# One hand-made instruction order across three stages, earlier page reads and split rotary angles in a two-layer block

## The chip, the core and the metric

The kernel runs on one core of one Trainium2 chip. The metric is the device time of one execution in microseconds (us). Everything is float32. PE is TensorE (matmul), DVE is VectorE, ACT is ScalarE, POOL is GpSimd, SP is SyncE; in this kernel SP does nothing but read a few indices and issue DMAs.

## The reference

There are eight sequences (B = 8) of 128 rows and 512 features. Layer 0 multiplies each sequence by one of eight adapter matrices and adds a small mixture of experts; layer 1 is an attention over a paged cache, followed by a gated bottleneck network. Cut to what matters here:

```python
# layer 0, per sequence b
c   = x[b] @ W0[adapter_id[b]].T
g   = c @ gate_w.T                       # 8 experts, the best 2, softmax
x1  = x[b] + c @ base_w.T + base_b + 2.0 * experts(c, g)

# layer 1, per sequence b
q, k, v = x1 @ Wq.T, x1 @ Wk.T, x1 @ Wv.T        # 32 query heads, 8 key heads, D = 128
pos     = cache_seqlens[b] + arange(128)
q, k    = rope(rmsnorm(q), pos), rope(rmsnorm(k), pos)   # cos/sin of pos * inv_freq
keys    = concat(k_cache[block_table[b]], k)     # 16 pages of 32 rows, then the new 128 rows
vals    = concat(v_cache[block_table[b]], v)
o       = softmax(q @ keys.T / sqrt(D), masked where cache row >= cache_seqlens[b]) @ vals
y       = o @ Wo.T
out     = x1 + gated_bottleneck(y)               # 64 gates, the best 16
```

## The kernel before

The program has three stages, each written in a `with` block of its own.

**Layer 0 (`l0`)** loops over the sequences, t = 0 to 7. In a pass PE multiplies by the adapter matrix (`l0_adapter`, L373, in two halves), DVE copies the result to `cT` (L382), PE multiplies `cT` by the gate and low-rank matrix `glw` (L390) and by `bww` (L395), DVE works out the gates (L401 to L419), and one pass later PE adds the experts (`l0_experts`, L437), DVE writes `x1` (L439), SP writes it to memory (`x1d`, L440) and PE transposes it (`l0_turn`, L447) into `x1T`. SP's queue loads, ahead of their pass, the adapter matrix `wt` (L284, three passes ahead), the transposed input `xT` and the input `xb`. In passes 2 to 7 SP also reads the cache pages of attention step 0 (`gather`, L151 for `kt` and L156 for `vt`), three pages a pass; a page is two DMAs of 64 KB. POOL's queue loads the projection weights (`load_q`, L129) and output weights (`load_o`, L134). After pass 1, `l0_angles` makes the rotary angles of all sequences on DVE (L345 to L361, ten instructions), and after pass 2 ACT makes `sin` and `cos` of them (L476, L477).

**Layer 1 (`l1`)** has 16 steps (a sequence and one half of the key heads) of four units each, 64 units. A unit is one key head with its four query heads. For a unit u: `project_q` (L195), `project_kv` (L208), `norms` (ACT's squares L224, POOL's `rs` L230), `rotate` (DVE, L242 to L255, into `ca`), a transposition (the first three units on PE, `transpose_qk` L634 with ACT's copy to `qkT` L638; the later ones through DVE and memory), `scores` (L660, L663), `mask_exp` (DVE L673, ACT L684), `normalize` (POOL L690), `blocks` (DVE L695), a transposition of the probabilities through memory (`exchange_out` L707 writes `px`, `exchange_in` L720 reads `pT`), `values` (L739) and `output` (L760). `make_mask` (DVE, L626) makes the mask of a step. Units 0 and 1 are projected and rotated at the end of `l0`; the first lines of `l1` are `transpose_qk(0)`, `project_q(2)`, `make_mask(0)`, `transpose_qk(1)`, `project_kv(2)`.

**The end (`l2`)** finishes the bottleneck network of the last sequences.

**What sets the order.** For SP's instructions one hand-made order holds for the whole program. For PE, DVE, ACT and POOL each of the first two stages has a hand-made order of its own (`l2` has one for PE, DVE and ACT), and where two stages meet a planner places the instructions. In the built program DVE's list at the seam of `l0` and `l1` reads: `mask` of step 0 (L626), then `rotate(0)`, then `rotate(1)`. An engine takes its list in order.

**Memory.** The tiles of `l1` (among them `mask` and `qkT`) take the place of the tiles of `l0`. So in the program's list of waits, `mask` of step 0 and `qkT` of unit 0 both wait for the last reader of that place, which is the DMA that writes `x1` of sequence 7 to memory (L440). `ca`, `rs`, `vn` and the tables lie elsewhere and have no such wait. SP's DMAs share eight semaphores in turn, so that an issue waits until the DMA eight before it has landed.

Of the kernel before, what the change touches and what calls it, by code (L numbers as in the profile page):

```python
# [9 lines left out]
F32 = mybir.dt.float32  # L10
I32 = mybir.dt.int32
AF = mybir.ActivationFunctionType
ALU = mybir.AluOpType
# [3 lines left out]
P = 128  # L17
B = 8
# [5 lines left out]
D = 128  # L24
HKV, REP = 8, 4
NH = REP + 1
PAGES, PSIZE, NPP = 64, 32, 16
# [16 lines left out]
PI_LOW = 3.1415925  # L44
INV_2PI = 0.15915494309189535
ROUND = 12582912.0

C1 = 6.28125
C2 = 0.0019340515136718750
C3 = 2.0 * PI - C1 - C2  # L50
# [3 lines left out]
def adaln_ffn_kernel(  # L54
# [23 lines left out]
):  # L78
    nc = tc.nc

    ctx.enter_context(tc.manual_schedule(engines={mybir.EngineType.SP}))
    const = ctx.enter_context(tc.tile_pool(name="const", bufs=1))
    keep = ctx.enter_context(tc.tile_pool(name="keep", bufs=1))
    wp = ctx.enter_context(tc.tile_pool(name="wp", bufs=GH))
# [9 lines left out]
    half_pi = const.tile([P, 1], F32, name="half_pi")  # L94
# [32 lines left out]
    def load_q(g, eng):  # L127
        t = wp.tile([P, NC, (REP + 2) * D], F32, tag="wqkv", name=f"wqkv_{g}")
        eng.dma_start(out=t, in_=wqkv[g].rearrange("(c p) n -> p c n", p=P))  # L129
        wq_t[g] = t  # L130
# [126 lines left out]


    with ExitStack() as l0:
        l0.enter_context(  # L260
            tc.manual_schedule(
                engines={
                    mybir.EngineType.PE,
                    mybir.EngineType.DVE,
                    mybir.EngineType.Activation,
                    mybir.EngineType.Pool,
                }
            )
        )
        w0p = l0.enter_context(tc.tile_pool(name="w0p", bufs=1))  # L270
        p2 = l0.enter_context(tc.tile_pool(name="l0_2", bufs=2))
        sm = l0.enter_context(tc.tile_pool(name="l0_s", bufs=2))
# [67 lines left out]
        fr = w0p.tile([P, D // 2], F32, name="fr")  # L340
        nc.gpsimd.dma_start(out=fr, in_=inv_freq.to_broadcast([P, D // 2]))

        def l0_angles():

            nc.vector.tensor_copy(lenf, leni)  # L345
            pos = w0p.tile([P, B], F32, name="pos")
            nc.vector.tensor_scalar(pos, lenf, pf, None, ALU.add)
            ang = yp.tile([P, B, D // 2], F32, tag="ya", name="ang")
            kk = yp.tile([P, B, D // 2], F32, tag="ya", name="kk")
            nc.vector.tensor_tensor(  # L350
                ang,
                pos.unsqueeze(2).to_broadcast([P, B, D // 2]),
                fr.unsqueeze(1).to_broadcast([P, B, D // 2]),
                ALU.mult,
            )
            nc.vector.tensor_scalar(kk, ang, INV_2PI, ROUND, ALU.mult, ALU.add)
            nc.vector.tensor_scalar(kk, kk, ROUND, None, ALU.subtract)
            for part in (C1, C2, C3):
                nc.vector.scalar_tensor_tensor(ang, kk, -part, ang, ALU.mult, ALU.add)
            nc.vector.tensor_scalar(ang, ang, PI_LOW, -PI_LOW, ALU.min, ALU.max)  # L360
            nc.vector.scalar_tensor_tensor(kk, ang, -1.0, ang, ALU.mult, ALU.max)  # L361
            return ang, kk

        state, cp_t, cT_t, lowT_t = {}, {}, {}, {}

# [88 lines left out]
        for t in range(B):  # L454
            l0_adapter(t, True)
            if t >= 1:
                l0_turn_low(t - 1)
            l0_adapter(t, False)
            if t + 3 < B:
                if t + 3 in (5, 6):  # L460
                    l0_home(t + 3)
                l0_load(t + 3)
            if t + 2 < B:
                l0_load_x(t + 2)
            if t >= 1:
                l0_experts(t - 1)
                if t in (3, 5, 7):
                    load_q((t - 3) // 2, nc.gpsimd)
            if t >= 2:
                gather(0, (t - 2) * 3, min((t - 1) * 3, NPP))  # L470
                l0_turn(t - 2)
            l0_base(t)
            if t == 1:
                angles = l0_angles()
            if t == 2:
                nc.scalar.activation(sin, angles[0], AF.Sin)  # L476
                nc.scalar.activation(cos, angles[1], AF.Sin, bias=half_pi, scale=-1.0)  # L477

        load_q(3, nc.gpsimd)
        for g in range(GH):  # L480
# [11 lines left out]
        project_kv(1)  # L492
        norms(1)
        rotate(1)
        gather(1, 0, 11)


    fw_t, zg_t = {}, {}
# [99 lines left out]


    with ExitStack() as l1:  # L600
        l1.enter_context(
            tc.manual_schedule(
                engines={
                    mybir.EngineType.PE,
                    mybir.EngineType.DVE,
                    mybir.EngineType.Activation,
                    mybir.EngineType.Pool,
                }
            )
        )  # L610
        wk1 = l1.enter_context(tc.tile_pool(name="l1_1", bufs=1))
        wk2 = l1.enter_context(tc.tile_pool(name="l1_2", bufs=2))
        pp = l1.enter_context(tc.tile_pool(name="l1_p", bufs=3))
# [203 lines left out]
        def iteration(u):  # L817

            on = lambda v: 0 <= v < NU
            fb = LAST.get(u)  # L820
            if on(u):
                st, k = units[u][0], units[u][1] % GH
                first, end = (0, 0, 6, 11)[k], (0, 6, 11, NPP)[k]
                if k > 0 and 1 < st + 1 < 2 * B:
                    gather(st + 1, first, first + 2)
            if on(u - 1):
                exchange_in(u - 1)
            if on(u) and k > 0 and 1 < st + 1 < 2 * B:
                gather(st + 1, first + 2, end)
            if u == 1:  # L830
                gather(1, 11)
            if on(u + 3) and units[u + 3][1] % GH == 0:
                make_tables(units[u + 3][0])
            if on(u - 1) and units[u - 1][1] == GH:
                load_y(units[u - 1][0])
            if on(u - 2):
                evict_o(u - 2)
            if u == NU:
                yT_t[fb] = f_turn(fb, *rooms[fb])
                z_turn(ORDER[0], bank("kv", "ztp_0"), rooms[ORDER[0]][0])  # L840
            if u == NU + 1:
                z_turn(ORDER[1], bank("q", "ztp_1"), rooms[ORDER[1]][0])
            for h in range(REP):
                if on(u):
                    scores(u, h)
                    mask_exp(u, h)
                    if h > 0:
                        normalize(u, h - 1)
                    if u == 1 and h == 1:

                        project_q(4)
                        transpose_qk(2)
                        project_kv(4)
                        rotate(3)
                        norms(4)
                    if h == 2:
                        new_pb(u)
                        if u + 2 in range(3, NU):
                            blocks_qk(u + 2, u)
                    if h > 1:  # L860
                        blocks(u, h - 2)
                    if h == 1 and u == NU - 3:
                        f_fold(rooms[fb][1])
                    if h == 2 and fb is not None:
                        yT_t[fb] = f_turn(fb, *rooms[fb])
                if on(u - 2):
                    output(u - 2, h)
            if on(u - 2):
                add_output(u - 2)
            if on(u + 1) and units[u + 1][1] % GH == 0:  # L870
                make_mask(units[u + 1][0])
            if on(u):
                normalize(u, REP - 1)
                blocks(u, REP - 2)
                blocks(u, REP - 1)
                exchange_out(u)
            if u == 0:
                project(3)
                rotate(2)
            elif u == 1:  # L880
                rotate(4)
            elif on(u + 3):
                project(u + 3)
                rotate(u + 3)
                if units[u + 3][0] == B - 1:
                    load_q(units[u + 3][1] + GH, nc.gpsimd)
            if u + 1 in range(3, NU):
                heads_qk(u + 1)
            if u == NU - 5:
                f_weights()  # L890
            if fb is not None:
                f_gate(fb, *f_project(fb, yT_t.pop(fb), *rooms[fb]), *rooms[fb])
            if on(u - 1):
                values(u - 1)
            if on(u - 2) and units[u - 2][0] == B - 1:
                load_o(units[u - 2][1] + GH, nc.gpsimd)
            if u in (NU - 3, NU - 2):
                load_y(B + u - (NU - 3))
            if NU - 4 <= u < NU:
                room(LAST[u + 1])  # L900
# [4 lines left out]
        transpose_qk(1)  # L905
        project_kv(2)
        norms(2)
        for u in range(NU + 2):
            iteration(u)


    with ExitStack() as l2:
        l2.enter_context(
            tc.manual_schedule(
                engines={
                    mybir.EngineType.PE,
                    mybir.EngineType.DVE,
                    mybir.EngineType.Activation,
                }
            )  # L920
        )
        p2 = l2.enter_context(tc.tile_pool(name="f_2", bufs=2))
        sm = l2.enter_context(tc.tile_pool(name="f_s", bufs=3))

# [152 lines left out]
```

## Time and profile before

| | |
|---|---|
| runs shown (3) | 1284.98 us median, 1283.83 to 1287.56 |
| profiled execution, its own time | 1285.63 us |
| its span, first to last instruction | 1283.9 us |
| PE busy | 1260.9 us (98%) |
| DVE busy | 783.3 us (61%) |
| ACT busy | 465.8 us (36%) |
| POOL busy | 342.0 us (27%) |
| mean granted TensorE clock | 0.997 |
| DMA | 293.15 MB, mean 228 GB/s |

The profile is one execution, 1.7 us of which lie around its span; it is 0.65 us above the median of the runs. A row of a timeline gives the start, the duration, the engine and line, the tiles (output <- inputs), how many instructions are merged, and in brackets the idle time of the engine before it and what ended that. "PEclk" is the TensorE clock that was granted, as a share of full speed. Matmuls are pipelined and their ends are modelled, so neighbouring rows overlap a little.

### The profile page before, as it was taken

Reading aid. Unit: us, or ns where it says so; the run is one execution under the profiler, and the core shown is the slowest. Engines: PE = TensorE matmul, PEld = TensorE weight load, DVE = VectorE, ACT = ScalarE, POOL = GpSimd, SP = SyncE. Lnnn points to the kernel's source line nnn. Section 1 sums busy time; section 2 is a strip of 40 time slices with the busy share of each in tenths; the row PEclk is TensorE's granted clock in tenths of the full one; section 3 lists DMA queues with packets and bytes.
Section 4 is the critical chain, followed back from the end, with each engine's and each line's share of the span. In section 5 each row is a group of like instructions: output and inputs, shape, how many; then the busy total and the mean of one; then the engine's idle time right before and its main releaser. Section 6 shows DMA issues by size and latency. Waiting matters only on the chain.

```text
span 1283.9 us, 15242 instructions
## 1 busy us (share of the span) xinstructions
PE 1260.9 (98%) x3949; PEld 670.4 (52%) x3949; DVE 783.3 (61%) x1794; ACT 465.8 (36%) x1397; POOL 342.0 (27%) x462
## 2 busy tenths in 40 slices
PE   8998999999999999999999999999999999999998
PEld 6665455555555555544555455555555555555545
DVE  3425666666666666656666566666666666665524
ACT  0214344334433443433343433433444444343211
POOL 2132232232323222323323222323232322221100
PEclk9999999999999999999999999999999999999999
DMA  8974667676767766699889776767767686786531
GB/s 307 305 269 123 215 208 240 198 248 226 221 217 239 228 219 223 228 284 294 277 267 291 231 232 226 236 226 224 246 215 233 207 260 204 234 276 214 187 107 49
DMA packets 176555, 293.15 MB, mean 228 GB/s; under 512 B 15971, under 2 KB 85924, under 8 KB 176468
## 3 DMA queue, kind: packets, MB, share of 16 engines
q1 hardware_dynamic: 153044, 218.83, 53.9%
q10 hardware_dynamic: 18960, 52.21, 11.7%
q0 software_dynamic: 4464, 21.14, 4.8%
q8 instruction: 31, 0.51, 0.2%
q14 instruction: 56, 0.46, 0.1%
HBM read 180.64 MB, written 111.48 MB: 228 GB/s over the span
## 4 chain that ended last, share of the span: by engine, by line
PE 88%; DMA 8%; DVE 2%; issue 1%; SPq 1%; POOL 0%; ACT 0%; ACTq 0%; DVEq 0%
PE o L739 21%; PE y L760 16%; PE s L660 15%; PE q L195 14%; PE kv L208 7%; DMA pT<-px 5%; PE s L663 4%; PE op L972 2%; PE bp L395 2%; PE cp L373 2%; DMA px<-pb 1%; PE fz L547 1%; PE fp L547 1%; DMA bww<-in_base_w 1%; PE cp L390 1%
## 5 line engine op out<-in xcount | busy, mean ns | idle before, releaser
L690 POOL TENSOR_SCALAR p<-p,den 128x640 f32<-128x640 f32 x256 | 204.3, 798 | 525.6 <-DVE den L689 525.6
L684 ACT ACTIVATE p<-p,low 128x640 f32<-128x640 f32 x256 | 212.1, 829 | 326.4 <-DVE den L689 231.4
L673 DVE CUSTOM_DVE_ANT_0 p<-s,mask,rs 128x640 f32<-128x640 f32 x256 | 226.2, 884 | 165.9 <-PE s L663 155.0
L760 PE MATMUL y<-wo,oT 128*128 128x512 f32 x512 | 261.4, 594 | 0.3 <-ACT oT L750 0.3
L660 PE MATMUL s<-kt,qkT 128*128 128x512 f32 x512 | 261.6, 592 | 0.0
L739 PE MATMUL o<-pT,vt 128*128 128x512 f32 x512 | 232.7, 597 | 7.7 <-DMA pT<-px 7.7
L195 PE MATMUL q<-wqkv,x1T 128*128 128x512 f32 x512 | 231.9, 596 | 0.0
L695 DVE STREAM_TRANSPOSE pb<-p 128x640 f32<-128x640 f32 x256 | 211.0, 824 | 11.7 <-POOL p L690 11.7
L663 PEld LDWEIGHTS s<-qkT 128*128 128x128 f32 x512 | 97.3, 190 | 122.5 <-issue 122.5
L195 PEld LDWEIGHTS q<-wqkv,x1T 128*128 128x128 f32 x512 | 97.6, 191 | 121.6 <-issue 121.6
L660 PEld LDWEIGHTS s<-kt,qkT 128*128 128x128 f32 x512 | 96.9, 190 | 118.8 <-issue 103.3
L739 PEld LDWEIGHTS o<-pT,vt 128*128 128x128 f32 x512 | 97.2, 191 | 108.3 <-issue 94.9
L224 ACT ACTIVATE sq<-q 128x128 f32<-128x128 f32 x256 | 71.0, 277 | 214.1 <-DVE pb L695 115.0
L242 DVE TENSOR_TENSOR ca<-q,tab 128x512 f32<-128x512 f32 x64 | 44.2, 690 | 165.0 <-ACT sq L224 162.0
L208 PE MATMUL kv<-wqkv,x1T 128*128 128x256 f32 x512 | 121.0, 379 | 0.0
L208 PEld LDWEIGHTS kv<-wqkv,x1T 128*128 128x128 f32 x512 | 97.0, 190 | 38.9 <-issue 29.0
L663 PE MATMUL s<-qkT 128*128 128x128 f32 x512 | 98.3, 274 | 0.0
L228 POOL TENSOR_SCALAR ss<-ss 128x5 f32<-128x5 f32 x64 | 12.6, 197 | 270.5 <-ACT sq L224 270.5
L750 ACT COPY oT<-o 128x512 f32<-128x512 f32 x64 | 37.4, 585 | 120.5 <-PE o L739 120.5
L760 PEld LDWEIGHTS y<-wo,oT 128*128 128x128 f32 x512 | 78.2, 192 | 3.6 <-issue 2.9
L230 POOL TENSOR_TENSOR rs<-ss,mhalf 128x5 f32<-128x5 f32 x64 | 75.4, 1179 | 5.3
L739 PE MATMUL o<-pT,vn 128*128 128x512 f32 x128 | 65.4, 592 | 0.0
(145 smaller groups left out, 953.9 us busy)
## 6 DMA issues: line engine op xcount, KB each, us to landing
pT<-px SPq DMA_DIRECT2D x64, 1280.0 KB, 7.1
px<-pb SPq DMA_DIRECT2D x122, 400.0 KB, 5.2
px<-pb ACTq DMA_DIRECT2D x122, 400.0 KB, 5.6
qkb<-px SPq DMA_DIRECT2D x61, 320.0 KB, 3.5
kt<-in_kc SPq DMA_DIRECT2D x256, 64.0 KB, 5.3
vt<-in_vc SPq DMA_DIRECT2D x256, 64.0 KB, 4.5
wqkv<-in_wqkv POOLq DMA_DIRECT2D x8, 1536.0 KB, 9.3
wo<-in_wo POOLq DMA_DIRECT2D x8, 1024.0 KB, 11.0
```

The source lines that it names most:

```text
L195: nc.tensor.matmul(out=q, lhsT=x1T[:, st % B, c, :], rhs=wq_t[g][:, c, : REP * D], start=(c == 0), stop=(c == NC - 1),)
L208: nc.tensor.matmul(out=kv, lhsT=x1T[:, st % B, c, :], rhs=wq_t[g][:, c, REP * D :], start=(c == 0), stop=(c == NC - 1),)
L224: nc.scalar.activation(sq, src, AF.Square, accum_out=ss[:, h : h + 1])
L230: nc.gpsimd.tensor_tensor(rs, ss, mhalf, ALU.pow)
L660: nc.tensor.matmul(out=s[:, :L], lhsT=qkT[:, h, :], rhs=kt[:, :, g % GH, :], start=True, stop=True)
L663: nc.tensor.matmul(out=s[:, L:NK], lhsT=qkT[:, h, :], rhs=qkT[:, REP, :], start=True, stop=True)
L673: nc.vector.tensor_tensor_reduce(out=p, in0=s_t.pop((u, h))[:, :NK], in1=mask_t[st], scale=rs_t[u][:, h : h + 1], scalar=BIG, op0=ALU.add, ...
L684: nc.scalar.activation(p, p, AF.Exp, bias=low, scale=-1.0, accum_out=den)
L690: nc.gpsimd.tensor_scalar(p_t[u, h], p_t[u, h], den, 1.0, ALU.mult, ALU.mult)
L695: nc.vector.transpose(pb_t[u][:, :, h * w : (h + 1) * w].rearrange("p i (j a) -> p j i a", a=32), p_t.pop((u, h)).rearrange("p (j i a) -> ...
L739: nc.tensor.matmul(out=o, lhsT=vt[:, c, j * D : (j + 1) * D] if c < LC else vn_t.pop(u), rhs=pT[:, c], start=(c == 0), stop=(c == LC),)
L760: nc.tensor.matmul(out=y_t[u], lhsT=oT_t[u][:, h, :], rhs=wo_t[g][:, h, :], start=(h == 0), stop=(h == REP - 1),)
```

## The change

The change has four parts. (1) One hand-made order now holds for all five engines over the whole program; the three orders of the stages are dropped. In the built program PE's list is the same as before. DVE's list at the seam becomes `rotate(0)`, `rotate(1)`, `mask`. On POOL, at the start, the instruction that finishes `ident` (the identity matrix) moves ahead of two small memsets and the DMA of `nw`. (2) `l0` reads four pages a pass instead of three: passes 2 to 5 read step 0's sixteen pages, passes 6 and 7 read the first eight of step 1. (3) Step 1's other eight pages are read at the start of `l1`, ahead of the first unit; before, eleven were read at the end of `l0` and five in unit 1, behind the `pT` read of unit 0. (4) `l0_angles` is cut in four: passes 1, 2 and 3 each make a part of DVE's work, and pass 4 makes ACT's `sin` and `cos`.

```diff
-    ctx.enter_context(tc.manual_schedule(engines={mybir.EngineType.SP}))
+    ctx.enter_context(
+        tc.manual_schedule(
+            engines={SP, PE, DVE, Activation, Pool}      # each as mybir.EngineType.*
+        )
+    )
...
-        l0.enter_context(tc.manual_schedule(engines={PE, DVE, Activation, Pool}))
...
+        ang = yp.tile([P, B, D // 2], F32, tag="ya", name="ang")
+        kk = yp.tile([P, B, D // 2], F32, tag="ya", name="kk")
-        def l0_angles():
+        def l0_angles(part):
+            if part == 0:
                 nc.vector.tensor_copy(lenf, leni)
                 pos = w0p.tile([P, B], F32, name="pos")
                 nc.vector.tensor_scalar(pos, lenf, pf, None, ALU.add)
                 nc.vector.tensor_tensor(ang, pos..., fr..., ALU.mult)
                 nc.vector.tensor_scalar(kk, ang, INV_2PI, ROUND, ALU.mult, ALU.add)
                 nc.vector.tensor_scalar(kk, kk, ROUND, None, ALU.subtract)
+            elif part == 1:
+                for c in (C1, C2, C3):
+                    nc.vector.scalar_tensor_tensor(ang, kk, -c, ang, ALU.mult, ALU.add)
+            elif part == 2:
                 nc.vector.tensor_scalar(ang, ang, PI_LOW, -PI_LOW, ALU.min, ALU.max)
                 nc.vector.scalar_tensor_tensor(kk, ang, -1.0, ang, ALU.mult, ALU.max)
+            else:
+                nc.scalar.activation(sin, ang, AF.Sin)
+                nc.scalar.activation(cos, kk, AF.Sin, bias=half_pi, scale=-1.0)
...
+            if 2 <= t <= 5:
+                gather(0, (t - 2) * 4, (t - 1) * 4)
+            elif t > 5:
+                gather(1, (t - 6) * 4, (t - 5) * 4)
             if t >= 2:
-                gather(0, (t - 2) * 3, min((t - 1) * 3, NPP))
                 l0_turn(t - 2)
             l0_base(t)
-            if t == 1:
-                angles = l0_angles()
-            if t == 2:
-                nc.scalar.activation(sin, angles[0], AF.Sin)
-                nc.scalar.activation(cos, angles[1], AF.Sin, bias=half_pi, scale=-1.0)
+            if 1 <= t <= 4:
+                l0_angles(t - 1)
...
         rotate(1)
-        gather(1, 0, 11)
...
-        l1.enter_context(tc.manual_schedule(engines={PE, DVE, Activation, Pool}))
...
-            if u == 1:
-                gather(1, 11)
...
         norms(2)
+        gather(1, 8)
         for u in range(NU + 2):
             iteration(u)
...
-        l2.enter_context(tc.manual_schedule(engines={PE, DVE, Activation}))
```

## The prediction

> **What bounds the kernel now.** I read the totals of the page first, then PE's waits, then the timelines of PE, DVE and SP around the largest of them, then the granted clock there.
>
> ```profile
> PE 1260.9 (98%) x3949; PEld 670.4 (52%) x3949; DVE 783.3 (61%) x1794; ACT 465.8 (36%) x1397; POOL 342.0 (27%) x462
> ...
> PE 88%; DMA 8%; DVE 2%; issue 1%; SPq 1%; POOL 0%; ACT 0%; ACTq 0%; DVEq 0%
> ```
>
> PE is the bound, and its list is not changed by a single matmul. So only 1283.9 - 1260.9 = 23.0 us of idle time, and what the clock loses after idle time, can be won. PE's waits say where it lies:
>
> ```profile
> PE o L739 <- DMA pT<-px: 7.7, 7, 2.7
> PE tq L634 <- DVE ca L255: 4.7, 1, 4.7
> PE cp L390 <- DVE cT L382: 2.6, 2, 1.8
> PE idle L453 <- POOL ident masks.py:199: 2.6, 1, 2.6
> ```
>
> (total us, times, longest.) The second and third, and the 2.7 us piece of the first, lie where the change works. DVE, then PE and SP, at the seam of the layers:
>
> ```profile
> 92.14 0.69 DVE L439 TENSOR_TENSOR x<-bp,xb 128x512 f32<-128x512 f32 x1 [6.74 <-PE bp L437]
> 99.48 0.55 DVE L626 TENSOR_SCALAR mask<-kidx,lenf 128x640 f32<-128x640 f32 x1 [6.66 <-DMA vt<-in_vc]
> 99.95 0.68 DVE L242 TENSOR_TENSOR ca<-q,tab 128x512 f32<-128x512 f32 x1
> ...
> 102.20 0.48 DVE L255 TENSOR_TENSOR ca<-ca,sa 128x320 f32<-128x320 f32 x1
> ```
> ```profile
> 96.19 1.89 PE L208 MATMUL kv<-wqkv,x1T 128*128 128x256 f32 x8
> 102.83 0.74 PE L634 MATMUL tq<-ident,ca 128*128 128x128 f32 x5 [4.75 <-DVE ca L255]
> 103.40 5.29 PE L195 MATMUL q<-wqkv,x1T 128*128 128x512 f32 x8
> 108.53 0.71 PE L634 MATMUL tq<-ident,ca 128*128 128x128 f32 x5
> ...
> 133.40 5.37 PE L739 MATMUL o<-pT,vt 128*128 128x512 f32 x8 [2.74 <-DMA pT<-px]
> ```
> ```profile
> 102.00:108.00 6.00, 5.17 (x12) 2.53 (x13) 3.38 (x8) 0.69 (x1) 0.00 (x0) 0.72 0.35 95
> ...
> 134.00:138.00 4.00, 4.00 (x7) 1.62 (x6) 3.64 (x8) 0.11 (x2) 0.86 (x2) 0.57 0.47 131
> ```
>
> DVE sits idle from 92.8 to 99.5 in front of `mask`. The row names a page read, but by the list of waits `mask` needs the write of `x1` of sequence 7, issued at 92.86 and landing 6.4 us later, at 99.3; the page read merely landed beside it. `rotate(0)`, whose inputs are there by 93.3 (`rs` ends 92.05 + 1.20), stands behind `mask` in DVE's list, and PE stands behind `rotate(0)`. The last fence gives the clock in its third number from the end: 0.72 and 0.57 after the two long waits. So a wait costs more than its length.
>
> **Angles split.** In pass 2 DVE makes all ten angle instructions (27.53 to 33.9) ahead of `cT` of sequence 2. PE has those matmuls at 31.4 and waits 1.78 us:
>
> ```profile
> 29.64 3.10 DVE L359 SCALAR_TENSOR_TENSOR ang<-kk,ang 128x512 f32<-128x512 f32 x3
> ...
> 34.59 1.19 PE L390 MATMUL cp<-glw,cT 128*128 128x136 f32 x8 [1.78 <-DVE cT L382]
> ```
>
> After, only the first five stand there (to 29.6), so `cT` follows PE directly: 1.78 us won. Part 1 (3.10) goes behind `low` of pass 2, which ends at 38.19 - 1.78 = 36.4, so it ends at 39.5; `cT` of sequence 3 can't start before 42.75 - 1.78 = 41.0, cover 1.5 us. Part 2 is 1.0 us from 46.8, needed free at 50.3. ACT's table load, `sin` and `cos` (36.79 to 39.2, 2.4 us) move two passes on; the next `lowT` there is ready 4.4 us after the `ex`, as the idle before the row at 59.88 shows, so 2.0 us are left. The reload (1.28) and its 1.14 us wait of DVE move likewise, and before them `low` was 1.6 us early for its transposition. All at nothing; if a cover fails, that slip is what PE waits.
>
> **The seam.** After, `rotate(0)` starts at 92.9, not 99.95, lasts 2.7 and ends near 95.7: PE's `tq` follows `kv` at 97.9 at once, and `project_q(2)` runs to 97.92 + 0.55 + 3.43 = 101.9 at full clock. `rotate(1)` now bounds: its `rs` is ready at 99.21 + 1.17 = 100.4, and from its third instruction to its last it takes 1.54 us (101.15 to 102.69 in `rotate(0)`), so the second `tq` starts near 102.1 instead of 108.70 on the chain: 6.6 us won, made of 4.75 idle, 1.69 of `q` (5.29 against 3.60) and small rest. ACT's `qkT`, moved by nothing, was covered by the old stall and now matters: it too waits for that write of `x1`. It must be done by 104.4, when `kv` of unit 2 ends, so the write may land up to 103.6.
>
> **The first `values`.** PE reaches it 21.9 us after the second `tq`, and `pT` came 24.7 after it (`px` 5.44, then `pT` 7.13 us). That chain moves up as a whole. Behind `pT`, SP issued five pages (127.3 to 135.1) which moved 0.64 MB beside its 1.28 MB; they are gone. A `pT` read takes 6.0 to 11.7 us in this trace, median 7.1, mostly with pages beside it. Ends: nothing won, or 1.1 of wait; I take 0.8, so a wait of 1.9.
>
> What of the clock? The trace has no loss after 1.78 us, none after 2.51 (709.32, eight matmuls in 3.70), and a loss after 2.74 (5.37 against 3.70, so 1.67). The Trainium skill, "TensorE: Matmul & The Clock Gate", Part 1, says that the clock halves after an idle window of about 3.4 us, windows running freely: by that the 2.74 us would keep full clock, the 1.67 had another cause and stays, and this part is worth 0.8. The trace has the clock at 0.57 right behind the wait, so I take the trace: 0.8 + 1.67 = 2.5. Ends of this part: 0 and 4.4.
>
> **Pages earlier.** Ahead of the write of `x1` of sequence 7, SP now issues 24 pages, not 16: 16 more DMAs and 1.05 MB in `l0`. Two pages more stand ahead of `wt` of sequence 7, and one ahead of that of 6. An issue waits for the DMA eight before; so one page read was held from 49.09 + 0.34 to 54.76 for `wt` of sequence 6. I let the queue slip 2.5 us: `wt` of 7 is issued near 58.9 (56.36 now), lands 8.7 later at 67.6, and PE wants it at 76.41 - 1.78 = 74.6: 7 us of cover. `xb` of sequence 6 comes at 68 instead of 65.7, and POOL's third `load_q` behind it at 69 instead of 66.97; its weights take 10 us and are wanted near 96. Nothing.
>
> The end of `l0` is tighter. While POOL's last loads run (80.5 to about 98), 64 KB pages issued at 82.8 took 9.1 us. With eight in flight that is 1.1 us a DMA, and between the writes of sequences 5 and 7 stand 17 DMAs: the last write may be issued at 95 instead of 91 (92.86 less 1.78). It then lands between 2.9 us later (an `xb` of the same size in quiet, 65.75) and 6.4 (as now): 93.9 to 101.4. In this shifted time it may land up to 103.6 - 1.8 = 101.8. The skill's "DMA: Bandwidth & Descriptors", Queues, rings and completion order, has the DMA engines take turns between queue rows packet by packet; by that 256 KB at half of the 400 GB/s seen there land in 1.3 us (an estimate from that page) and nothing is near the edge. The trace's 6.4 us decides; I charge 0.5, ends 0 and 1. The eight pages behind it need 1.36 us each (93.71 to 95.09), end near 107, and `px` of unit 0 wants SP at 120.2 - 8.4 = 111.8. Step 1's keys are wanted only in unit 4, near 174 us (unit 3's scores start at 156.8, a unit takes 17.2).
>
> **POOL's start.** `ident` is ready about 1.2 us sooner (2.20 becomes about 1.0), so the 22 warming transposes end near 6.3 and PE idles 1.9 us, not 0.69, until the first weights at 8.20. By the row of 1.78 no clock is lost; if it is, half speed for 3.6 us of work costs 1.7, of which 0.87 lies before `bww` lands. I take 0; ends 0 and -0.9.
>
> **Sum.** 1.78 + 6.6 + 2.5 - 0.5 = 10.4 us. The profiled execution took 1285.63, so 1275.2; the median of the runs is 0.65 below it: 1274.6. Ends: 1.78 + 6.6 + 0 - 1 - 0.9 = 6.5 (1278.5), and 1.78 + 6.6 + 4.4 = 12.8 (1272.2).
>
> **Rivals.**
> - *The write of `x1` takes the stall back.* If SP's queue is worse than reckoned and the write lands at 105, `qkT` comes at 105.8 instead of 102.6: PE waits 3.2 us and perhaps loses 1.7 of clock; the gain is 5.5 to 7, so about 1279. For: 9.1 us a page under load. Against: POOL's loads end near 98. Chance 0.14.
> - *The gain is given back later.* The five `pT` waits between 560 and 710 us, 4.6 us of the 7.7, come of DMA load in that stage; the runs shown spread over 3.7 us. If they grow by 6 or more: 1281 to 1286. Nothing in them is touched. 0.07.
> - *The change doesn't do what it says:* if DVE's new order does not free `rotate(0)`, because it waited for something else, 2 to 4 us remain: 1282. Against: `rs` was there at 93.3. 0.01.
> - *Slower:* the pages ahead of `wt` of sequence 7 starve PE at L373 of pass 7. It is wanted at 74.6 and was there at 65.1: 9.5 us of slip cost nothing, and up to 10.4 + 3.9 more are paid by the gain or can't be told from noise; it decides from about 24 us. Two pages held 5.7 us each, the longest hold seen, give 11.4. At 25 to 30 us of slip: 1290. 0.03.
>
> **How the numbers follow.** The main case (0.75) gives 1274.6, own range 1272.2 to 1278.5. The runs scatter by about 0.3%, 3.9 us, which is what a measurement can tell from no change: faster means below 1281.1. The range of 8 in 10 takes a microsecond more below and the first rival's 1279 to 1280 above: 1271.2 to 1280. Faster: 0.75 + 0.14 + a little of the second = 0.91; same 0.06; slower 0.03.
>
> **What would show it.** Right: DVE goes from `x` of sequence 7 to `ca` without a wait; PE's wait at L634 is below 0.5 us; the second `tq` lies 8.4 us earlier; L390's longest wait is 0.8; the clock is 1.00 between 96 and 130 us; the wait at the first L739 is about 1.9 us, with eight matmuls in 3.70. Wrong: a wait at L660 for `qkT` (the first rival), at L373 (the last), or `pT` waits after 500 us above 6 us in total.

## The result and the profile after

Over eleven runs of each kernel beside one another the changed kernel takes 1275.61 us in the median (1269.1 to 1283.03), the kernel before 1286.62 (1283.83 to 1291.14): a ratio of 0.992, 95% interval 0.9896 to 0.9943, so 11.0 us by the medians. The whole interval lies more than 0.3% below 1, so it is faster. 1274.6 was forecast, and 10.4 us.

The profiled execution of the changed kernel took 1278.66 us, three above its median, with a span of 1276.9 us (1283.9 before). The totals, then PE's waits:

```profile
PE 1260.5 (99%) x3949; PEld 671.8 (53%) x3949; DVE 781.8 (61%) x1794; ACT 465.7 (36%) x1397; POOL 342.1 (27%) x462
...
PE 91%; DMA 6%; DVE 1%; issue 0%; SPq 0%; ACT 0%; POOL 0%; ACTq 0%; DVEq 0%
```
```profile
PE o L734 <- DMA pT<-px: 5.3, 3, 3.4
PE cp L379 <- DMA wt<-in_w: 2.6, 1, 2.6
PE o L734 <- DVE den L684: 2.5, 1, 2.5
PE idle L459 <- POOL half_pi L105: 1.4, 1, 1.4
PE cp L396 <- DVE cT L388: 0.8, 1, 0.8
```

(The lines have moved: L373 is L379 now, L390 L396, L634 L629, L660 L655, L739 L734.) The 4.75 us wait for `ca` is gone, and of the waits for `cT` the 1.78 us one. A new one stands in the second row: 2.6 us in front of the first weights. DVE at the seam, SP's write of `x1` and first `pT` read, then ACT, and PE from there to the first `values`:

```profile
90.73 0.69 DVE L445 TENSOR_TENSOR x<-bp,xb 128x512 f32<-128x512 f32 x1 [6.73 <-PE bp L443]
91.33 0.68 DVE L252 TENSOR_TENSOR ca<-q,tab 128x512 f32<-128x512 f32 x1
...
102.35 0.55 DVE L621 TENSOR_SCALAR mask<-kidx,lenf 128x640 f32<-128x640 f32 x1 [1.81 <-DMA kt<-in_kc]
```
```profile
94.05 0.33 SPq L446 DMA_DIRECT2D x1d<-x  x1
...
119.04 0.63 SPq L715 DMA_DIRECT2D pT<-px  x1
```
```profile
102.31 1.29 ACT L633 COPY qkT<-tq 128x640 f32<-128x640 f32 x2 [4.72 <-DMA kt<-in_kc]
```
```profile
96.51 0.71 PE L629 MATMUL tq<-ident,ca 128*128 128x128 f32 x5
97.06 3.60 PE L205 MATMUL q<-wqkv,x1T 128*128 128x512 f32 x8
100.69 0.74 PE L629 MATMUL tq<-ident,ca 128*128 128x128 f32 x5
101.27 1.89 PE L218 MATMUL kv<-wqkv,x1T 128*128 128x256 f32 x8
103.05 1.12 PE L655 MATMUL s<-kt,qkT 128*128 128x512 f32 x2
...
125.53 3.67 PE L734 MATMUL o<-pT,vt 128*128 128x512 f32 x8 [2.52 <-DVE den L684]
```

`rotate(0)` follows `x` of sequence 7 without a gap, PE goes through the seam at full clock, and the second `tq` starts at 100.69 instead of 108.53. `mask` and `qkT` still wait for the write of `x1`, which now lands at 102.13, 2.9 us later than before. (Their rows name a page read, `kt`, that landed beside it. But `mask` starts 0.22 us after the landing of the write before, here and in e2 below, and `qkT` 0.18 us after it here, in e4 and in e6, wherever the write falls.) `mask` has time. `qkT` just has it: the first of its two copies ends at 103.00, and the first score starts at 103.05, 2.36 us behind the second `tq`; with an early write it is 2.30 (e7). The row of the first `values` names DVE's `den`, but as in e7 and e11, whose rows name `pT`, PE starts 0.13 us after the `pT` read has landed (125.40), so I count it as a wait for `pT`.

At the start of the program and late in it, time is lost:

```profile
1.36 4.60 PE L459 MATMUL idle<-ident 128*128 128x128 f32 x22 [1.36 <-POOL half_pi L105]
8.53 5.44 PE L379 MATMUL cp<-xT,wt 128*128 128x128 f32 x32 [2.56 <-DMA wt<-in_w]
...
15.78 3.60 PE L401 MATMUL bp<-bww,cT 128*128 128x512 f32 x8
...
699.62 6.45 PE L734 MATMUL o<-pT,vt 128*128 128x512 f32 x8 [3.42 <-DMA pT<-px]
```

I follow the first score of unit 2 (139.46 us before, 129.90 after) as a mark: 9.56 us are won up to there. Between the two spans 7.0 us are left, so 2.6 are given back behind it. The later waits for `pT` cost 4.99 us before (six waits) and now 5.3 (1.50, 3.42 and 0.36), and the longest of them 2.75 of clock besides (6.45 against 3.70). These late losses vary from run to run. Of the eleven runs of the changed kernel, the four with a granted clock of 0.999 or more took 1269.1 to 1274.87 us, the seven with 0.997 or less 1274.09 to 1283.03. So two profiled executions don't give the difference of the medians.

### The profile page after: what moved, and what is told of

It reads as the page before. It is cut to its first block, busy times and chain, and to the rows that moved or that the text cites. A ratio compares the mean times of both kernels' runs of the same rounds, so it can differ in the third digit from the quotient of the medians.

```text
span 1276.9 us, 15242 instructions
## 1 busy us (share of the span) xinstructions
PE 1260.5 (99%) x3949; PEld 671.8 (53%) x3949; DVE 781.8 (61%) x1794; ACT 465.7 (36%) x1397; POOL 342.1 (27%) x462
## 4 chain that ended last, share of the span: by engine, by line
PE 91%; DMA 6%; DVE 1%; issue 0%; SPq 0%; ACT 0%; POOL 0%; ACTq 0%; DVEq 0%
PE o L734 21%; PE s L655 16%; PE y L755 16%; PE q L205 15%; PE kv L218 8%; PE s L658 4%; DMA pT<-px 4%; PE cp L379 2%; PE op L957 2%; PE bp L401 2%; DMA px<-pb 2%; PE fz L552 1%; PE fp L552 1%; PE cp L396 1%; PE bp L443 1%; DMA wt<-in_w 0%
## 5 line engine op out<-in xcount | busy, mean ns | idle before, releaser
L655 PE MATMUL s<-kt,qkT 128*128 128x512 f32 x512 | 261.7, 593 | 0.0
L734 PE MATMUL o<-pT,vt 128*128 128x512 f32 x512 | 233.6, 599 | 7.9 <-DMA pT<-px 5.3
L655 PEld LDWEIGHTS s<-kt,qkT 128*128 128x128 f32 x512 | 96.8, 190 | 119.0 <-issue 102.9
L734 PEld LDWEIGHTS o<-pT,vt 128*128 128x128 f32 x512 | 97.8, 192 | 108.4 <-issue 95.4
L734 PE MATMUL o<-pT,vn 128*128 128x512 f32 x128 | 65.4, 592 | 0.0
```

The costliest lines, as they stand in the source:

```text
L655: nc.tensor.matmul(out=s[:, :L], lhsT=qkT[:, h, :], rhs=kt[:, :, g % GH, :], start=True, stop=True)
L734: nc.tensor.matmul(out=o, lhsT=vt[:, c, j * D : (j + 1) * D] if c < LC else vn_t.pop(u), rhs=pT[:, c], start=(c == 0), stop=(c == LC),)
```

## The experiments

The times of before differ a little from one set of runs to the next, so a timed kernel is given as a ratio to before, measured beside it. The position of the mark comes from each kernel's trace.

**e1: the order alone.** Single order as in the change; the angles whole, the pages as before.

```diff
-            if 1 <= t <= 4:
-                l0_angles(t - 1)
+            if t == 1:
+                l0_angles(0); l0_angles(1); l0_angles(2)
+            if t == 2:
+                l0_angles(3)
...
+                gather(0, (t - 2) * 3, min((t - 1) * 3, NPP))    # t >= 2; and 11 pages at the
+        gather(1, 0, 11)                                          # end of l0, 5 in unit 1
```

> One hand-made order for the whole program and nothing else: the rotary angles whole in pass 1 and the pages read as before (three a pass, eleven at the end of l0, five in unit 1). Theory (the gain is mask moved behind the rotations on DVE): PE's wait of 4.75 us for ca and the slow q behind it are gone; the second tq starts near 102.7 us (108.70 before, 100.69 after), the 1.78 us wait for cT of sequence 2 stays; the first score of unit 2 starts near 132 us (139.46 before, 129.90 after); time about 1277.5 us, 8 to 9 us under before. Rival (the early page reads or the spread angles free the seam): the wait for ca stays above 4 us, and the time is within 3 us of before.

Measured: ratio 0.9939 (0.9915 to 0.9962), 1280.84 us. PE's timeline:

```profile
34.45 2.04 PE L396 MATMUL cp<-glw,cT 128*128 128x136 f32 x8 [1.95 <-DVE cT L388]
...
103.66 0.73 PE L631 MATMUL tq<-ident,ca 128*128 128x128 f32 x5
...
128.64 3.67 PE L736 MATMUL o<-pT,vt 128*128 128x512 f32 x8 [2.83 <-DMA pT<-px]
```

The wait for `ca` is gone with the order alone, the wait for `cT` stays, and the second `tq` comes at 103.66 (102.7 forecast; behind the wait of 1.95 us the clock was down, 0.53 over the next 3.5 us). The mark comes at 133.01 (132 forecast), 6.45 of the 9.56 us. By the medians the time is 7.3 us under before, a little less than the 8 to 9 forecast. The order is the larger part of the gain, 0.6% of 0.8%, though the two intervals overlap. The rival falls.

**e2: `mask` back in front of the rotations**, the rest as in the changed kernel.

```diff
-        rotate(0)                # in l0, behind l0_turn(B - 2)
-        rotate(1)                # in l0, behind norms(1)
...
+        make_mask(0)             # first lines of l1
+        rotate(0)
+        rotate(1)
         transpose_qk(0)
         project_q(2)
-        make_mask(0)
```

> The changed kernel with DVE's order at the seam as it was before: mask of step 0, rotate(0), rotate(1). Theory: mask waits for the write of x1 of sequence 7, which the earlier page reads have made late (it landed at 102.3 us in the changed kernel, 99.3 before), so the wait of PE for ca is longer than before, about 9 us from 96.6 to 105.7, with a slow q behind it; the second tq starts near 111 us, later than the 108.70 of before; time about 1287 us, no better than before. Rival (mask's place is harmless, something else in the change won the time): the second tq stays near 100.7 and the time near 1275.6.

Measured: ratio 0.9996 (0.9985 to 1.0007), 1287.17 us: the whole gain is gone. DVE, then PE:

```profile
100.21 0.55 DVE L619 TENSOR_SCALAR mask<-kidx,lenf 128x640 f32<-128x640 f32 x1 [10.44 <-DMA kt<-in_kc]
```
```profile
103.55 1.30 PE L627 MATMUL tq<-ident,ca 128*128 128x128 f32 x5 [8.53 <-DVE ca L265]
104.64 5.89 PE L205 MATMUL q<-wqkv,x1T 128*128 128x512 f32 x8
110.37 0.71 PE L627 MATMUL tq<-ident,ca 128*128 128x128 f32 x5
```

One instruction, in its old place, costs 8.5 us of waiting and 2.3 of clock (5.89 against 3.60), more than the 4.75 of before. The earlier pages have made the write late: SP issued it at 92.94, 3.2 us after `x` was ready, where before it went out at once. The parts of the change are not independent: the pages would have made the old order worse.

**e3: the angles whole**, the rest as in the changed kernel (the first half of e1's edit).

> The changed kernel with the angles whole, all ten DVE instructions behind pass 1 and sin and cos behind pass 2, as before. Theory: the wait of PE for cT of sequence 2 is back, 1.8 us, and everything behind it slips by as much: the second tq near 102.5 us, the first score of unit 2 near 131.7 us; time 1.8 us over the changed kernel, 1277.4. Rival (the slip is swallowed by the late write of x1 or by the first pT): the first score of unit 2 stays within 0.5 us of 129.90.

Measured: ratio 0.9928 (0.99 to 0.9956), which can't be told from the changed kernel's 0.992. The trace can tell:

```profile
35.45 1.53 PE L396 MATMUL cp<-glw,cT 128*128 128x136 f32 x8 [2.48 <-DVE cT L388]
36.77 5.00 PE L401 MATMUL bp<-bww,cT 128*128 128x512 f32 x8
```

The wait is back and longer than in the kernel before, and this time it took clock with it (5.00 against 3.60). The second `tq` starts at 104.66, 4.0 us later than in the changed kernel, where 1.8 were forecast: 2.48 of wait and some 1.8 of clock, less 0.46 for weights that landed earlier. Splitting the angles takes away a wait that was 1.8 to 2.5 us long in the three profiles that have it (before, e1, e3), and with it the clock that two of these lost.

**e4: the pages as before**, the rest as in the changed kernel (the second half of e1's edit).

> The changed kernel with the page reads as before: three a pass, eleven of step 1 at the end of l0, five in unit 1. Theory (the page reads are hidden either way): the write of x1 of sequence 7 is issued at 91 us, not 94, and lands before 99, so qkT of unit 0 starts near 99 instead of 102.3; PE gains nothing from it at the second tq (100.7); the first pT has five pages beside it again; the first score of unit 2 within 0.7 us of 129.90; time within 2 us of the changed kernel. Rival (the early pages are part of the gain): the first values waits 1 us longer or loses clock, so 1 to 3 us slower than the changed kernel.

Measured: ratio 0.9903 (0.987 to 0.9936), 1277.11 us. ACT, SP, then PE:

```profile
97.44 0.69 ACT L631 COPY qkT<-tq 128x640 f32<-128x640 f32 x1 [0.33 <-DMA kt<-in_kc]
```
```profile
117.91 0.63 SPq L713 DMA_DIRECT2D pT<-px  x1
```
```profile
100.22 0.74 PE L627 MATMUL tq<-ident,ca 128*128 128x128 f32 x5
...
125.14 5.25 PE L732 MATMUL o<-pT,vt 128*128 128x512 f32 x8 [2.77 <-DMA pT<-px]
```

The write is issued at 90.97 and `qkT` starts 4.9 us sooner, which wins PE nothing. The wait at the first `values` is 2.77 us, 0.25 longer than in the changed kernel, and here it cost clock. That 0.25 is a difference of two effects. The five pages beside the `pT` read lengthen it: from its issue to the first `values` it is 7.23 us here and 6.49 in the changed kernel. The early write shortens the chain ahead of it (e7). The page reads' move wins nothing that the times show.

**e5: 34 warming transposes instead of 22**, the rest as in the changed kernel.

> The changed kernel with 34 warming transposes on PE instead of 22. In the changed kernel they end at 6.0 us and PE idles 2.56 us until the first weights at 8.53, and the first 32 matmuls then take 5.44 us instead of 3.81. Theory (the earlier identity matrix opened that gap and the gap costs the clock): the gap is under 1 us, the 32 matmuls take 3.8 us at a clock of 1.00, the first bp follows the landing of bww near 14.9 instead of 15.78, and all behind it is about 0.7 to 0.9 us earlier. Rival (the matmuls are slow because the weights come late): they take above 5 us again.

```profile
1.37 5.92 PE L459 MATMUL idle<-ident 128*128 128x128 f32 x34 [1.37 <-POOL half_pi L105]
8.23 3.85 PE L379 MATMUL cp<-xT,wt 128*128 128x128 f32 x32 [0.95 <-DMA wt<-in_w]
12.87 1.19 PE L396 MATMUL cp<-glw,cT 128*128 128x136 f32 x8 [0.78 <-DVE cT L388]
14.20 3.70 PE L401 MATMUL bp<-bww,cT 128*128 128x512 f32 x8
```

The gap falls to 0.95 us, the first matmuls run at full speed, and `bp` starts at 14.20 instead of 15.78. The earlier `ident` had opened the gap, as the theory said. But the gap does not always cost the clock: of the eight profiles with the early `ident` and 22 transposes, e2 and e6 (gaps of 1.76 and 1.58 us) had the 32 matmuls in 3.83 and 3.94 us, the other six (1.50 to 2.56) in 5.20 to 5.44. One run took 1276.88 us; a difference of this size isn't to be seen in one.

**e6: all sixteen pages of step 1 in passes 6 and 7.**

```diff
             elif t > 5:
-                gather(1, (t - 6) * 4, (t - 5) * 4)
+                gather(1, (t - 6) * 8, (t - 5) * 8)
...
-        gather(1, 8)
```

> The changed kernel with all sixteen pages of step 1 read in passes 6 and 7, eight a pass, so that eight more pages stand ahead of the write of x1 of sequence 7 in SP's queue. Theory (that write is the edge of the seam): it is issued 8 us later, near 102, and lands near 105 to 107, so qkT of unit 0 starts there; PE waits 3 to 4 us at the first score, perhaps with a slow stretch behind it; first score of unit 2 near 134 us (129.90); time 3 to 6 us over the changed kernel. Rival (the write is covered by norms and the rotations): first score of unit 2 within 0.7 us of 129.90.

Measured: ratio 1.0012 (0.9995 to 1.003), 1287.41 us: eight pages more ahead of one write undo the change. SP, ACT and PE:

```profile
106.48 0.37 SPq L446 DMA_DIRECT2D x1d<-x  x1
```
```profile
108.86 1.29 ACT L633 COPY qkT<-tq 128x640 f32<-128x640 f32 x2 [13.39 <-DMA x1d<-x]
```
```profile
109.60 2.07 PE L655 MATMUL s<-kt,qkT 128*128 128x512 f32 x2 [8.56 <-ACT qkT L633]
```

The write was issued 12.4 us later (94.05 in the changed kernel), not 8, and PE waited 8.56 us for `qkT`, not 3 to 4. The mechanism is that of the theory, its size was forecast too small: the write of sequence 6, eight pages earlier in the queue, had slipped as well (to 92.21).

**e7: the four pages of pass 7 behind the write.**

> The changed kernel with the four pages of pass 7 moved behind the write of x1 of sequence 7. Theory (in the changed kernel the late write just meets its cover): the write is issued near 92 us instead of 94.05 and lands near 98, qkT of unit 0 starts before 99.5 instead of 102.31, PE's first score is not earlier (103.05), the chain of the first pT is 0.4 us shorter since ACT does the squares of unit 2 sooner, and the wait at the first values falls from 2.52 to about 2.1 us. Rival (the write costs PE something now): the first score comes more than 0.5 us earlier relative to the second tq.

```profile
97.39 0.69 ACT L633 COPY qkT<-tq 128x640 f32<-128x640 f32 x1
```
```profile
100.38 0.74 PE L629 MATMUL tq<-ident,ca 128*128 128x128 f32 x5
102.68 1.02 PE L655 MATMUL s<-kt,qkT 128*128 128x512 f32 x2
...
124.64 5.37 PE L734 MATMUL o<-pT,vt 128*128 128x512 f32 x8 [2.11 <-DMA pT<-px]
```

`qkT` comes at 97.39, the first score 2.30 us behind the second `tq` (2.36 in the changed kernel), and the wait at `values` is 2.11 instead of 2.52. So the late write costs PE 0.06 us at the score, and 0.4 us at `values`; the theory has that come through ACT, whose squares of unit 2 stand behind `qkT` (they start at 101.74 here, at 103.48 in the changed kernel). The `pT` read is as short as in the changed kernel: 6.47 us from its issue to `values`. The shorter wait cost clock here (5.37); the longer one had not. One run: 1276.54 us.

**e9: 34 transposes, the write first, and the first `values` moved behind two scores of unit 2.**

```diff
+                if u == 2 and h == 1:
+                    values(0)
+                    evict_o(0)
-                if on(u - 2):
+                if on(u - 2) and u != 2:      # unit 0's outputs follow the fourth score
                     output(u - 2, h)
```

> 34 warming transposes, the write of x1 of sequence 7 ahead of the pages, and the first values placed behind the first two scores of unit 2, its outputs behind the fourth. Theory (PE's wait for the first pT is a matter of its place only): the two scores, 2.2 us of PE, fill the wait; what stays of it is below 0.5 us and there is no clock to lose; unit 2's projection ends about 2.5 us earlier relative to the second tq than in the changed kernel; the clock is 1.00 from 8 to 500 us. Rival (pT is later by as much, since the masks and exponentials of the two scores come first): the wait stays near 2 us.

```profile
123.71 1.12 PE L655 MATMUL s<-kt,qkT 128*128 128x512 f32 x2 [1.23 <-DVE low L668]
124.90 3.60 PE L734 MATMUL o<-pT,vt 128*128 128x512 f32 x8
130.11 1.12 PE L655 MATMUL s<-kt,qkT 128*128 128x512 f32 x2 [0.76 <-DVE low L668]
```

`values` waits no longer, but the scores wait, 1.23 and 0.76 us, for DVE to free their buffers. From the second `tq` to the next projection behind unit 2 it is 36.86 us (99.08 to 135.94), against 36.97 in the changed kernel (100.69 to 137.66): 0.1 us, not 2.5. So the forecast failed, though not as the rival had it: the wait moved from `values` to the scores. That points to DVE's work on the scores as the bound of this stretch, which no run here tests. What was kept is the clock (1.00 from 8 to 500 us). One run took 1274.92 us. Timed later, beside e10:

> e9 again, timed. Theory: the 1.6 us of clock at the start and 1.7 us at the first values are never lost, so the median lies 1 to 3 us below that of the changed kernel timed beside it, about 1273.5, and the granted clock is 0.999 or more in most runs. Rival (those losses are rare in the changed kernel's timed runs): the medians agree within 1 us.

Ratio 0.99 (0.9874 to 0.9927), 1273.47 us, 1 to 3 us below the changed kernel as forecast (2.7, though the intervals overlap); five of six runs had a clock of 0.999 or 1.000. The changed kernel beside it:

> The changed kernel once more, beside the two others. Expected: 1274 to 1278 us, runs spread over 10 us, the runs with a clock of 0.999 or more near 1273 and those at 0.997 or less near 1279.

Ratio 0.9918 (0.9895 to 0.9941), 1276.2 us (1274.82 to 1277.91), the three runs at 0.999 at 1274.82 to 1276.14, the three at 0.997 or less at 1276.26 to 1277.91: the same order as forecast, but much closer together.

**e10: e9, and the weight loads of the second half in four parts each.** The profiles showed what still stood between every version and a PE without waits: `pT` reads between 560 and 720 us.

```diff
-                if units[u + 3][0] == B - 1:
-                    load_q(units[u + 3][1] + GH, nc.gpsimd)          # 1.5 MB at once
+                if on(u) and on(u + 2) and units[u + 2][0] == B - 1:
+                    load_q_part(units[u + 2][1] + GH, h)             # 384 KB a head
-                load_o(units[u - 2][1] + GH, nc.gpsimd)
+                    load_o_part(units[u - 3][1] + GH, h)             # likewise, 256 KB
```

> The kernel with 34 warming transposes, the write first and values behind two scores (e9), and each projection and output weight load of the second half (1.5 and 1 MB, between 560 and 720 us) cut into four, one part a head of the following unit. Theory (the pT waits there come from those loads' bursts, and the clock lost behind them is a part of the scatter): the waits for pT are below 1.5 us in total instead of 4.7, none above 1 us; clock 1.00 in nearly every run; time about 1268 us, 5 to 7 us below the changed kernel on the same chip, with less scatter. Rival (the reads of pages and pT alone fill the DMA there): the waits stay above 4 us and the time equals e9's.

Measured: ratio 0.9869 (0.9844 to 0.9894), 1269.56 us, five runs within 1269.26 and 1270.73, all with a clock of 1.000. DMA issues between 545 and 720 us, of e9 as timed and of e10, then e10's waits of PE:

```profile
pT<-px SPq DMA_DIRECT2D x10, 1280.0 KB, 9.3
```
```profile
pT<-px SPq DMA_DIRECT2D x10, 1280.0 KB, 7.4
wqkv<-in_wqkv POOLq DMA_DIRECT2D x15, 384.0 KB, 4.8
```
```profile
PE s L667 <- DVE low L680: 2.0, 2, 1.2
PE cp L391 <- DMA wt<-in_w: 1.7, 1, 1.7
...
PE o L746 <- DMA pT<-px: 1.0, 1, 1.0
```

The same bytes, in smaller parts and spread over time, let a `pT` read land in 7.4 us instead of 9.3; its waits fall from 4.5 us to 1.0 in all. Whether it is the size of the parts or their spread was not tested apart. This version beats both kernels, and its slowest run is faster than the fastest of e9 beside it (1270.9).

## Why the prediction was right

**The mechanism and the sum.** The time, its direction and the largest cause were right. By the terms of the sum, up to the mark at the first score of unit 2 (9.56 us won in the two profiled executions, 10.4 forecast):

- *Angles, 1.78.* PE meets `cT` of sequence 2 without a wait. The start of L396 moved from 34.59 to 33.28, 1.31 us: within 0.2 us the forecast less the 0.64 lost before it (below). The covers for the later parts held: no wait for `cT` of sequences 3 or 4, nor for `lowT`.
- *The seam, 6.6.* From that L396 to the second `tq` it was 73.94 us before and is 67.41: 6.5 us. `rotate(1)` bounds it through its `rs`, as forecast (98.97 to 99.01). e1 and e2 show that `mask`'s place is the cause, and with `rotate(0)` behind `x` without a gap the third rival falls.
- *First `values`, 2.5, and late write, 0.5.* The two meet at the same wait: 2.0 net was forecast, and from the second `tq` to the mark it is 30.93 us before and 29.21 after, 1.72. The pages' part held: from the issue of the `pT` read to `values` it is 7.26 us before (126.14 to 133.40) and 7.23 in e4, with five pages beside it, and 6.49 in the changed kernel and 6.47 in e7, without: 0.75, where 0.8 was forecast. The late write took back 0.4 of it (e7), so the wait fell from 2.74 to 2.52, not to 1.9. The clock was kept, 1.70 of this term; that was luck, and not won by a shorter wait. It was kept at 2.83 us in e1 and lost at 2.11 in e7 and, in the changed kernel itself, at 2.29 in e11. The prediction read a threshold out of four waits; there is none in that range.
- *The write itself.* It was forecast to be issued between 91 and 95 and to land by 101.4, with room to 101.8. Issued at 94.05, it landed at 102.13, 8.1 us after, 0.7 beyond the forecast's end. With the 0.64 us from the start, PE's first score had its operand just in time (0.06 us late). e6 shows what lay beyond the edge.
- *Start, 0 with an end of -0.9.* The gap grew to 2.56 us and cost clock; `bp` of sequence 0 came 0.93 us later, and 0.64 were left one pass on. The bound held, the value taken did not: with 0.64 of the 0.8 us that the mark fell short, this is the term that was most off. e5 takes it away.

**The rivals.** The first, the write taking the stall back, did not come, but no room was left; e6 brought it about with eight more pages. The second, a gain given back at the late `pT` waits, came by 2.6 us in the profiled pair, and by chance: in e11's profile the waits behind the first `values` are 4.9 us, as before, and none of them cost clock. That the medians differ by 11.0 us all the same has to do with before's runs, which lose clock as well: of the fifteen beside e5 to e9, those at 0.993 took 1287.74 to 1288.87 us, those at 0.997 1282.7 to 1284.58. The slow case did not come: no wait at L379 in pass 7.

## What to carry to other kernels

Where two stages of a program meet, read each engine's built list for an instruction whose wait is for a buffer, not for data: moving it behind work that is ready was most of this gain, and e2 shows that with it in front the rest is worth nothing. Before a transfer is moved earlier in a queue, ask what else in that queue releases memory, and how much room it has: here it was all used up. When PE is at 98%, the short waits that are left cost their length and at times nearly as much again in clock, so many small waits removed (e10) steady the time as well as shorten it.

## What the runs showed of the hardware

The clock behind a wait is not set by the wait's length alone. At 2.51, 2.52, 2.59, 2.83 and 3.11 us of waiting (before, after, e3, e1, e9) the matmuls behind ran at a granted clock of 1.00. At 1.95, 2.02, 2.10, 2.11 and 2.29 us (e1, e6, e5, e7, e11) it was 0.50 to 0.69 over the next three microseconds, and eight matmuls of 512 took 5.37 us instead of 3.70 at four of these. A wait of 2.59 us kept it in e3 and lost it in e5, and the five waits of 3.42 us and more (3.42, 3.58, 4.75, 8.53, 8.56) all lost it. Two waits of the same kernel at the same place (2.52 in the changed kernel's first profile, 2.29 in its second) fell on either side. This fits an idle window that runs freely, as the Trainium skill has it ("TensorE: Matmul & The Clock Gate", Part 1), but not one that has to be wholly idle for its 3.4 us. What phase decides was not measured.
